# Column recurrence and directional maxima scheduled as one region, with reordered stores and a new opening of the last stage

## The chip, the cores and the metric

The kernel runs on one core of one Trainium2 chip. A core has five engines with their own instruction streams: TensorE (PE, matrix products), VectorE (DVE), ScalarE (ACT, functions of one variable), GpSimd (POOL) and SyncE (SP, which here only issues transfers). Sixteen DMA engines move data between the chip's memory and the core's on-chip memory; a transfer is issued from the instruction stream of SP, ACT or POOL. Engines wait for each other by semaphores. The metric is device time in microseconds (us) of one execution of the whole kernel, given as the median of several runs.

## The reference

The input is an image tensor of 8 × 32 × 256 × 256 (batch, channels, rows, columns) in 32-bit floating point. Four layers follow each other; each adds its result to its input, and each works on an input normalised in 16 groups of channels (`_gn`: mean and variance of an image's two channels over all pixels).

```python
x = x + _L0_conv_ref(_gn(x), w1r, w1i, w2r, w2i, bias)      # spectral convolution, 32 x 32 low modes
x = x + _L1_conv_ref(_gn(x), kernel, 1, 2)                  # 5x5 convolution, one kernel for all channels
x = x + _L2_conv_ref(_gn(x), w_ih, b_ih, w_hh, b_hh)        # recurrence over the columns
x = x + _L3_conv_ref(_gn(x), W, b)                          # running maxima in four directions, 1x1 mix
```

The recurrence goes over the 256 columns from left to right. Column 0 is its own state; for each later one, with `x` the three neighbouring rows of the state before:

```python
r = sigmoid(r_i + r_h); z = sigmoid(z_i + z_h)
n = tanh(n_i + r * n_h)
new = n * z + cur_col * (1.0 - z)
```

The last layer takes the normalised input and its running maxima downwards, upwards, to the right and to the left, and mixes these 5 × 32 channels to 32.

## The kernel before

`forward_and_mix` does the forward transform and the mixing of the modes, and stores spectra in a scratch tensor `smd` in the chip's memory. `inverse_and_conv` transforms back, adds, normalises and convolves, in 16 units (image, half of the channels); its output goes to the scratch tensor `x2d` through `store` (L546 to L559), each half unit in twelve transfers: four groups of rows, each with its inner columns, its first 30 columns and its last columns. It reads its inputs as tiles `xb` (loads on POOL, L388) and `spec` (on SP or ACT, L351 and L353). `statistics` and `keep` make the mean and scale of each group into `stb` (copies, L591) with a power on POOL (L583). After the last unit, `keep(n - 1, statistics(n - 1))` comes before `store(n - 1, 1)`, whose transfers are shared between SP and ACT. The first 8 columns of images 0 to 6 are loaded early into a tile `first` (POOL, L678).

`recurrence` takes the columns in 32 blocks of 8. A column is worked on in two half steps, four images each (510 half steps after column 0). For a block, `load` (L739) brings eight tiles of `x2d` on SP; the load of the last image of `first` is on SP too (L746). `normalise` (L752, ACT) scales and shifts half a block of one image. The statistics reach all partitions by a transpose into `turned` (L726) and become `shift` (L730). In a half step PE forms r, z and n of the gates (`within` L772, `across` L780); ACT takes the two sigmoids (`rs` L847, `zm` L849, `zs` L850) and the tanh (L854), DVE makes n (L848, L853), the product with z (L859) and the new state `hs` (L861), POOL the product with 1 - z (`a`, L856) and the sum with the layer's input (L862), which is written over the raw columns. `running` keeps the running maximum to the right (`fm`, L883) and stores it to the scratch tensor `fwd`; `finish` stores the layer's output to `x3d` and takes its statistics (`bst`, L894). Both stores use `store` (L868 to L875): SP, but POOL for the last block's `fwd`. The order of the whole loop is written out by hand (`manual_schedule`); what lies before and behind is ordered by a scheduler.

`maxima_and_mix` goes over the same 32 blocks from right to left, block 31 first. It loads a block of `x3d` (tile `x3`) and of `fwd` (tile `fw`) on SP (`load`, L999). DVE forms the maxima of pairs of row groups (L1033), their maximum `top` (L1035), two scans down and up the rows (`dq` L1037, `uq` L1039), the maxima `m` (L1041, L1043, L1045), and, between these, the eight steps of the running maximum to the left (`back`, `rv`, a copy at L1029 for the rightmost column and L1031 for the others). PE mixes (L1062), ACT adds the bias while it moves results to the tile `ot` (L1077) and issues its store. Ahead of the loop stand the statistics (L921 to L925, L63 to L71, L950 to L957), the bias `bres` (L980, L981) and the constants `cuts`, `top`, `sel` and `wsum`, all on DVE but for the power (L71, POOL).

Tiles live in pools, which are opened and closed as stages begin and end. Where a pool takes the place of an earlier one, its tiles wait until what was there is done with. Transfers issued by SP and ACT take turns on eight semaphores, so that each waits for the one eight before it.

Of the kernel before, what the change touches and what calls it, by code (L numbers as in the profile page):

```python
# [296 lines left out]
def inverse_and_conv(tc, k, d, smd, xmean, x2d, stb, first):  # L297
# [16 lines left out]
    with ExitStack() as ctx:  # L314
        one = ctx.enter_context(tc.tile_pool(name="a2c", bufs=1))
        xp = ctx.enter_context(tc.tile_pool(name="a2x", bufs=1))
        wk = ctx.enter_context(tc.tile_pool(name="a2w", bufs=2))
        sm = ctx.enter_context(tc.tile_pool(name="a2s", bufs=3))
# [226 lines left out]
        def store(u, ch):  # L545
            b, h = units[u]  # L546
            c0 = 2 * CH * h + CH * ch
            x1, to = x1_of(u, ch), x2d[b, :, :, c0 : c0 + CH].rearrange("w a c q -> w a (c q)")
            for a in range(A):
                r = 32 * a  # L550
                queue = nc.scalar if a % 2 and 2 * u + ch == 2 * n - 1 else nc.sync
                queue.dma_start(
                    out=to[TS + 2 : TS * (NT - 1) + 2, a].rearrange("(t w) n -> w t n", w=TS),
                    in_=x1[r + 2 : r + 30, 2:NT].rearrange("w t c q -> w t (c q)"),
                )
                queue.dma_start(out=to[0 : TS + 2, a], in_=x1[r : r + 30, 1].rearrange("w c q -> w (c q)"))
                queue.dma_start(
                    out=to[TS * (NT - 1) + 2 : W, a], in_=x1[r + 2 : r + 32, 0].rearrange("w c q -> w (c q)")
                )  # L559
# [49 lines left out]
        with tc.manual_schedule(engines=None):  # L609
# [21 lines left out]
            for u in range(n):  # L631
# [47 lines left out]
                if more:  # L679
                    squares(u + 1, 1, 1, 1, NT)  # L680
            keep(n - 1, statistics(n - 1))
            store(n - 1, 1)
# [20 lines left out]
def recurrence(tc, k, d, x2d, x3d, fwd, stb, first, loaded, mean1, mv3):  # L703
# [10 lines left out]
    with ExitStack() as ctx:  # L714
        one = ctx.enter_context(tc.tile_pool(name="bc", bufs=1))
        blk = ctx.enter_context(tc.tile_pool(name="bb", bufs=2))
        wk = ctx.enter_context(tc.tile_pool(name="bw", bufs=2))
# [15 lines left out]
        for t in hs[0] + hs[1]:  # L733
            nc.vector.memset(t, 0.0)
# [4 lines left out]
        def load(bi):  # L739
            if bi:  # L740
                t = blk.tile([P, B, WB, Q], F32, name=f"xw_{bi}", tag="xw", bufs=4)
                for b in range(B):
                    nc.sync.dma_start(out=t[:, b], in_=columns(x2d, b, bi * WB, (bi + 1) * WB))
            else:
                t = first
                nc.sync.dma_start(out=t[:, B - 1], in_=columns(x2d, B - 1, 0, 8))  # L746
            raws[bi] = t
            norms[bi] = blk.tile([P, B, WB, Q], F32, name=f"xn_{bi}", tag="xn")

        def normalise(bi, b, half):  # L750
            w = slice(half * WB // 2, (half + 1) * WB // 2)
            nc.scalar.activation(  # L752
                norms[bi][:, b, w], raws[bi][:, b, w], AF.Identity, bias=shift[:, b : b + 1], scale=sc[:, 1, b : b + 1]
            )
# [71 lines left out]
        def step(w, x):  # L826
# [6 lines left out]
            else:  # L833
# [22 lines left out]
                product = nc.gpsimd.tensor_tensor(a, zm, cur, ALU.mult)  # L856
                if pieces[x]:
# [10 lines left out]
        def store(bi, dst, t):  # L868

            for a in range(A):  # L870
                for b2 in range(2):
                    (nc.gpsimd if bi == NB - 1 and dst is fwd else nc.sync).dma_start(
                        out=dst[bi, :, a, b2].rearrange("(i c) n -> c i n", c=C),
                        in_=t[rows(a), 4 * b2 : 4 * b2 + 4].rearrange("p i w q -> p i (w q)"),
# [14 lines left out]
        def finish(bi):  # L889
            raw = raws[bi]  # L890
            store(bi, x3d, raw)
# [5 lines left out]
        with tc.manual_schedule(engines=None):  # L897
            load(0)
            load(1)
            for half in range(2):  # L900
                for b in range(B):
                    normalise(0, b, half)
            for bi in range(NB):
                for wi in range(WB):
                    if wi == WB // 2 and bi + 2 < NB:
                        load(bi + 2)
                    for x in range(NC):
                        step(bi * WB + wi, x)
                        if bi + 1 < NB:
                            half, b = divmod(NC * wi + x, B)  # L910
                            normalise(bi + 1, b, half)
                    running(bi, wi)
                finish(bi)
# [4 lines left out]
        parts = bst.rearrange("p b n (h k) -> p b (n h) k", k=3)  # L918
        n = 2 * NB
        second = one.tile([P, B, n], F32, name="second")  # L920
        nc.vector.tensor_tensor(second, parts[:, :, :, 1], parts[:, :, :, 1], ALU.mult)  # L921
        nc.vector.scalar_tensor_tensor(second, parts[:, :, :, 2], n / float(W * Q), second, ALU.mult, ALU.add)
        nc.vector.tensor_reduce(mv3[:, :, 0], parts[:, :, :, 1], AX.X, ALU.add)
        nc.vector.tensor_reduce(mv3[:, :, 1], second, AX.X, ALU.add)
        nc.vector.tensor_scalar_mul(mv3, mv3, 1.0 / n)  # L925


def maxima_and_mix(tc, k, d, x3d, fwd, mv3, mean1, out):
# [4 lines left out]
    NB = W // WB  # L933
    with ExitStack() as ctx:
        one = ctx.enter_context(tc.tile_pool(name="cc", bufs=1))
        blk = ctx.enter_context(tc.tile_pool(name="cb", bufs=2))
        op = ctx.enter_context(tc.tile_pool(name="co", bufs=3))
        ps = ctx.enter_context(tc.tile_pool(name="cp", bufs=2, space=PSUM))
# [5 lines left out]


        sta, _ = finish_stats(tc, one, ps, k, mv3, B, k.pair, "c", "o1", 2)
        st = one.tile([P, 2, 2], F32, name="st3")
        for i in range(4):
            q = slice(32 * i, 32 * i + 32)
            nc.vector.tensor_copy(st[q], sta[q, i::4, :])  # L950
        shift = one.tile([P, 2], F32, name="shift3")
        nc.vector.scalar_tensor_tensor(shift, st[:, :, 0], -1.0, st[:, :, 1], ALU.mult, ALU.mult)
        wsc = one.tile([P, 2, 5, C], F32, name="wsc")
        for b2 in range(2):
            nc.vector.tensor_scalar_mul(wsc[:, b2], w3, st[:, b2, 1:2])

            nc.vector.tensor_tensor(wsc[:, b2, 0], wsc[:, b2, 0], k.ident32, ALU.add)  # L957


        wsum = one.tile([P, A, C], F32, name="wsum")  # L960
        nc.vector.tensor_tensor(wsum[:, 0], w3[:, 0], w3[:, 1], ALU.add)
        for t in range(2, 5):
            nc.vector.tensor_tensor(wsum[:, 0], wsum[:, 0], w3[:, t], ALU.add)
        for j in range(1, A):
            nc.vector.tensor_copy(wsum[:, j], wsum[:, 0])
        sel = one.tile([P, 2, 4], F32, name="sel")
        nc.vector.memset(sel, 0.0)
        for i in range(4):
            q = slice(32 * i, 32 * i + 32)
            nc.vector.tensor_copy(sel[q, :, i], shift[q])  # L970
        bp = ps.tile([P, 2, 4], F32, name="bp", tag="o0")
        nc.tensor.matmul(
            bp.rearrange("p b i -> p (b i)"),
            lhsT=wsum.rearrange("p j o -> p (j o)"),
            rhs=sel.rearrange("p b i -> p (b i)"),
            start=True,
            stop=True,
        )
        bres = one.tile([P, 2, 4], F32, name="bres")
        nc.vector.tensor_scalar_add(bres, bp, b3[:, 0:1])  # L980
        nc.vector.tensor_tensor(bres, bres, mean1.rearrange("p (b i) -> p b i", b=2), ALU.add)  # L981


        QP = Q + 2
        cuts = one.tile([P, 2, 2 * WB, QP], F32, name="cuts")
        nc.vector.memset(cuts, BIG)
        nc.vector.memset(cuts[:, 0, :, 0:1], -BIG)
        nc.vector.memset(cuts[:, 1, :, QP - 1 : QP], -BIG)
        cutf = cuts.rearrange("p s w q -> p s (w q)")
        top = one.tile([P, 2, WB, QP], F32, name="top")  # L990
        nc.vector.memset(top, -BIG)

        xs = {}

        def load(bi):

            for src, tag, n in ((x3d, "x3", A + 2), (fwd, "fw", A)):
# [221 lines left out]
```

## Time and profile before

| | us |
|---|---|
| median of 3 runs | 3059.18 |
| lowest and highest run | 3055.52, 3066.23 |
| the profiled execution's own time | 3042.76 |
| its span in the trace | 3041.0 |
| first stage | 0 to 293 |
| first matmul of the convolution's stage | 316.63 |
| last matmuls of that stage's statistics | 997 |
| first sigmoid of the recurrence | 1020.50 |
| last `hs` of the recurrence | 2376.29 |
| first maximum of the last stage (L1033) | 2405.08 |
| from there to the end | 636 |

In the profile, busy times of an engine are sums over its instructions, without those that only wait or issue transfers. "PEclk" or "granted clock" is the share of full speed that PE was given. A row of a timeline has start, duration, engine, line, operation, output and inputs, and in brackets how long the engine had stood before it and what it waited for. A row of the chain has start, length and what the end of the execution hung on in that time; a part called DMA is a transfer under way, "SPq" the issuing of one. The profiled execution is 16.4 us (0.5%) below the median of the runs.

### The profile page before, as it was taken

How to read it: one execution, taken by the hardware profiler on the slowest of the kernel's cores; microseconds unless marked ns; L12 is line 12 of the kernel's file. 1: busy time of each engine (PE TensorE's matmuls, PEld its weight loads, DVE VectorE, ACT ScalarE, POOL GpSimd, SP SyncE). 2: the span in 40 equal slices, each digit the busy share in tenths (PEclk: the TensorE clock that was granted, in tenths of full speed). 3: DMA queues.
4: the chain of work that ended last, by engine and by line, in shares of the span. 5: the costliest groups of instructions: out<-in, count | busy, mean ns of one | idle time of the engine just before them, and what ended most of it. 6: DMA issues, size and time to landing. Idle time of an engine off the chain costs nothing.

```text
span 3041.0 us, 111672 instructions
## 1 busy us (share of the span) xinstructions
PE 2787.3 (92%) x47736; PEld 1644.8 (54%) x47736; DVE 2580.6 (85%) x5172; ACT 1868.2 (61%) x4482; POOL 874.4 (29%) x1253
## 2 busy tenths in 40 slices
PE   7986799999999799999999999999999488888887
PEld 4666344444445466666666666666666233333333
DVE  5753688888888699999999999999999799999997
ACT  3432477777677678888888888888887122222222
POOL 0110022211121355555555555555555200000000
PEclk9995899999999899999999999999999799999988
DMA  9977677877765566566666667656674688888885
GB/s 380 392 282 220 202 223 232 240 230 219 230 209 163 140 152 165 142 141 146 165 160 144 141 146 168 157 141 142 150 168 113 205 325 325 324 326 329 333 332 224
DMA packets 468193, 655.69 MB, mean 216 GB/s; under 512 B 328784, under 2 KB 329696, under 8 KB 441456
## 3 DMA queue, kind: packets, MB, share of 16 engines
q1 hardware_dynamic: 407528, 487.89, 55.1%
q0 software_dynamic: 16784, 84.11, 8.3%
q10 hardware_dynamic: 43384, 76.55, 7.0%
q8 instruction: 374, 6.13, 0.8%
q14 instruction: 123, 1.01, 0.1%
HBM read 371.63 MB, written 272.63 MB: 212 GB/s over the span
## 4 chain that ended last, share of the span: by engine, by line
PE 71%; DVE 20%; issue 4%; DMA 3%; ACT 1%; SPq 0%; POOL 0%; ACTq 0%; DVEq 0%; POOLq 0%
PE r L772 14%; PE z L772 13%; PE vp L498 13%; PE ni L772 7%; PE nh L772 6%; PE up L427 4%; DVE rv L1031 4%; PE yp L131 3%; DVE dq L1037 2%; DVE uq L1039 2%; DVE m L1045 2%; DVE m L1043 2%; DVE m L1041 2%; PE sp L158 2%; PE tp L410 2%
## 5 line engine op out<-in xcount | busy, mean ns | idle before, releaser
L780 PE MATMUL z<-hs,weights 64*64 64x256 f32 x4080 | 539.4, 382 | 0.0
L780 PE MATMUL r<-hs,weights 64*64 64x256 f32 x4080 | 525.4, 375 | 0.0
L780 PE MATMUL ni<-hs,weights 64*64 64x256 f32 x4080 | 524.9, 375 | 0.0
L862 POOL TENSOR_TENSOR xw<-xw,hs 128x256 f32<-128x256 f32 x496 | 339.9, 685 | 635.8 <-DVE hs L861 634.1
L1077 ACT ACTIVATE ot<-o,bres 128x512 f32<-128x512 f32 x256 | 154.9, 688 | 505.5 <-PE o L1062 490.1
L531 DVE SCALAR_TENSOR_TENSOR x<-vp,r,x 128x128 f32<-128x128 f32 (+2 forms) x640 | 350.6, 563 | 90.5 <-PE vp L498 78.2
L498 PE MATMUL vp<-x,c_conv 64*64 64x384 f32 (+5 forms) x4608 | 422.1, 490 | 2.4 <-DVE x L531 2.4
L854 ACT ACTIVATE n<-n,bih 128x256 f32<-128x256 f32 x510 | 259.2, 508 | 187.8 <-DVE n L853 187.8
L856 POOL TENSOR_TENSOR a<-zm,xn 128x256 f32<-128x256 f32 x510 | 372.3, 730 | 6.4 <-ACT zm L849 6.1
L1062 PE MATMUL o<-m,wsc 32*32 32x512 f32 x3072 | 230.5, 728 | 108.7 <-DVE m L1045 103.7
L772 PE MATMUL r<-hs,weights 64*64 64x256 f32 x2040 | 319.0, 389 | 5.1 <-DVE hs L861 4.2
L772 PE MATMUL z<-xn,weights 64*64 64x256 f32 x2040 | 305.3, 376 | 15.2 <-DMA xw<-x2d 15.2
L498 PEld LDWEIGHTS vp<-x,c_conv 64*64 64x64 f32 x4608 | 221.7, 132 | 172.6 <-issue 93.8
L772 PE MATMUL r<-xn,weights 64*64 64x256 f32 x2040 | 305.7, 377 | 0.8 <-ACT rs L847 0.8
L772 PE MATMUL nh<-xn,weights 64*64 64x256 f32 x2040 | 305.7, 376 | 0.0
L772 PE MATMUL z<-hs,weights 64*64 64x256 f32 x2040 | 305.2, 376 | 0.0
L772 PE MATMUL ni<-hs,weights 64*64 64x256 f32 x2040 | 305.2, 376 | 0.0
L752 ACT ACTIVATE xn<-xw,shift,turned 128x256 f32<-128x256 f32 x496 | 290.6, 586 | 0.0
L848 DVE SCALAR_TENSOR_TENSOR n<-nh,bhh,rs 128x256 f32<-128x256 f32 x510 | 246.3, 483 | 45.8 <-ACT rs L847 31.6
L780 PEld LDWEIGHTS ni<-hs,weights 64*64 64x64 f32 x4080 | 284.5, 133 | 0.3
L780 PEld LDWEIGHTS r<-hs,weights 64*64 64x64 f32 x4080 | 281.2, 131 | 0.2
L847 ACT ACTIVATE rs<-r,brz 128x256 f32<-128x256 f32 x510 | 241.3, 473 | 53.1 <-PE r L780 32.5
(166 smaller groups left out, 6245.0 us busy)
## 6 DMA issues: line engine op xcount, KB each, us to landing
xb<-in_xl_dram POOLq DMA_DIRECT2D x96, 768.0 KB, 7.5
xa<-in_xt_dram SPq DMA_DIRECT2D x64, 1024.0 KB
x<-x3d SPq DMA_DIRECT2D x32, 2048.0 KB
fw<-fwd SPq DMA_DIRECT2D x32, 2048.0 KB
out_dram<-ot ACTq DMA_DIRECT2D x64, 1024.0 KB
xw<-x2d SPq DMA_DIRECT2D x248, 256.0 KB
fwd<-fm SPq DMA_DIRECT2D x248, 256.0 KB
x3d<-xw SPq DMA_DIRECT2D x248, 256.0 KB
```

The source lines that it names most:

```text
L498: ins = nc.tensor.matmul(vps[bank][to, :, dst], lhsT=k.conv[r, P : P + 64] if kind == 2 else k.conv[r, o], rhs=pair_of(u, ch, g, lo, hi, s ...
L531: nc.vector.scalar_tensor_tensor(x, src[o], r1[rows, g : g + 1], x, ALU.mult, ALU.add, accum_out=s1[rows, 0, n, ch, g : g + 1])
L752: nc.scalar.activation(norms[bi][:, b, w], raws[bi][:, b, w], AF.Identity, bias=shift[:, b : b + 1], scale=sc[:, 1, b : b + 1])
L772: ins = nc.tensor.matmul(out[r], lhsT=weights[r, kind, gate, :], rhs=src[r], start=start, stop=stop)
L780: ins = nc.tensor.matmul(out[pairs[1 - i]], lhsT=weights[r, kind, gate, :], rhs=prev[r, :, q0 : q0 + Q], start=False, stop=stop,)
L847: rs = nc.scalar.activation(r, p["r"], AF.Sigmoid, bias=brz[:, 0:1])
L848: nc.vector.scalar_tensor_tensor(m, p["nh"], bhh[:, 2:3], r, ALU.add, ALU.mult)
L854: nc.scalar.activation(m, m, AF.Tanh, bias=bih[:, 2:3])
L856: product = nc.gpsimd.tensor_tensor(a, zm, cur, ALU.mult)
L862: nc.gpsimd.tensor_tensor(raw, raw, new, ALU.add)
L1062: nc.tensor.matmul(pts[b2][i][32 * j : 32 * j + 32].rearrange("p (w q) -> p w q", q=Q), lhsT=wsc[q, b2, t, :], rhs=src[j][q, b2], start=first,
L1077: nc.scalar.activation(ot[:, i], pts[b2][i], AF.Identity, bias=bres[:, b2, i : i + 1])
```

## The change

In `inverse_and_conv` the pool `a2c` is opened after `a2x` and `a2w`. `store` issues all its transfers on SP and the first columns ahead of the inner ones; for the last half unit it is ordered by parts, all first columns, then all inner, then all last. It is now called ahead of the statistics, behind a small sigmoid on ACT, and the load of the last image of `first` follows it on POOL.

In `recurrence` the tiles lie in more pools, which wait by the bytes that a tile covers (`reuse_waits="tile"`) and not for the whole of what lay there. Only the edges of `hs` are cleared. `normalise` can go to POOL: the second half of block 0 for images 0 to 3 before the first step, for images 4 to 7 in half steps 2 to 5, and the first half of block 1 for images 0 to 3 in half steps 8 to 11. The last block's `x3d` is stored in three parts (columns 0 to 3, 4 to 5, 6 to 7), and its `fwd` on SP.

The last stage is put into the same hand-ordered region. It loads block 30 first, then block 31 (both on ACT), and begins with maxima of block 30 between the steps of the statistics. Block 31's steps come in between; block 30 is finished before block 31's `m`. From block 29 on the order is that of before. The constants are made on POOL.

```diff
-        one = ctx.enter_context(tc.tile_pool(name="a2c", bufs=1))
         xp = ctx.enter_context(tc.tile_pool(name="a2x", bufs=1))
         wk = ctx.enter_context(tc.tile_pool(name="a2w", bufs=2))
+        one = ctx.enter_context(tc.tile_pool(name="a2c", bufs=1))
...
-                queue = nc.scalar if a % 2 and 2 * u + ch == 2 * n - 1 else nc.sync
...
+            last = 2 * u + ch == 2 * n - 1
+            parts = [(a, part) for a in range(A) for part in range(3)]
+            for a, part in sorted(parts, key=lambda x: x[1]) if last else parts:
+                r, queue = 32 * a, nc.sync
+                if part == 0:
+                    queue.dma_start(out=to[0 : TS + 2, a], in_=x1[r : r + 30, 1].rearrange("w c q -> w (c q)"))
...
+            nc.scalar.activation(junk[:, 0, 0:1], k.mhalf[:, 0:1], AF.Sigmoid)
+            store(n - 1, 1)
+            nc.gpsimd.dma_start(out=first[:, B - 1], in_=columns(x2d, B - 1, 0, 8))
             keep(n - 1, statistics(n - 1))
-            store(n - 1, 1)
...
+        one = ctx.enter_context(tc.tile_pool(name="bc", bufs=1, reuse_waits="tile"))
+        xnp = ctx.enter_context(tc.tile_pool(name="bn", bufs=2, reuse_waits="tile"))
+        xws = {i: ctx.enter_context(tc.tile_pool(name=f"bx{i}", bufs=1, reuse_waits="tile")) for i in (0, 3, 1, 2)}
...
-            nc.vector.memset(t, 0.0)
+            nc.vector.memset(t[:, :, 0 : Q + 2 : Q + 1], 0.0)
...
-                nc.sync.dma_start(out=t[:, B - 1], in_=columns(x2d, B - 1, 0, 8))
...
+            if other:
+                nc.gpsimd.tensor_scalar(
+                    norms[bi][:, b, w], raws[bi][:, b, w], sc[:, 1, b : b + 1], shift[:, b : b + 1], ALU.mult, ALU.add
+                )
+                return
...
                 product = nc.gpsimd.tensor_tensor(a, zm, cur, ALU.mult)
+                if extra:
+                    normalise(*extra, True)
...
-            store(bi, x3d, raw)
+            store(bi, x3d, raw, 6 if bi == NB - 1 else 0)
...
-            for half in range(2):
-                for b in range(B):
-                    normalise(0, b, half)
+            for b in range(B):
+                normalise(0, b, 0)
+            for b in range(BC):
+                normalise(0, b, 1, True)
+            other = {2 + b: (0, BC + b, 1) for b in range(BC)}
+            other.update({8 + b: (1, b, 0) for b in range(BC)})
...
+                    if bi == NB - 1 and wi in (3, 5):
+                        store(bi, x3d, raws[bi], wi - 3 if wi == 3 else 4, wi + 1)
...
-            load(NB - 1)
-            for bi in range(NB - 1, -1, -1):
+            load_x(NB - 2, nc.scalar)
+            load_x(NB - 1, nc.scalar)
+            load_f(NB - 2, nc.scalar)
+            load_f(NB - 1, nc.sync)
+            constants()
+            sums()
+            order("m10")
+            variance()
+            order("m11 m12")
+            scales()
+            order("m13")
+            biases()
+            order("m14 b07 b06 m15 b05 b04 m16 b03 b02")
+            known(NB - 2)
+            order("m00 b01 b00 m01 b17 b16 b15 b14 m02 b13 b12 m03 b11 b10")
+            finish(NB - 2)
+            load_x(NB - 3, nc.sync)
+            load_f(NB - 3, nc.sync)
+            order("m04 m05 m06")
+            known(NB - 1)
+            finish(NB - 1)
+            for bi in range(NB - 3, -1, -1):
```

In a word of `order`, "m" is one of the seven maxima of a block (0: pairs, 1: `top`, 2 and 3: the scans, 4 to 6: the three `m`) and "b" a step to the left; the first digit is the block counted from 31 downwards, the second the maximum or the column. `known` issues the products of four of the five inputs, `finish` those of the maximum to the left, the bias and the output's store.

## The prediction

> **What bounds the kernel now.** I read the page's slices first: PE 9 to 10 tenths through the convolution and the recurrence, DVE and DMA 8 to 9 tenths after it, and dips between. Then busy times by stretch, to put a price on each stage and each dip.
>
> ```profile
> core 0: us, PE busy (x) PEld busy (x) DVE busy (x) ACT busy (x) POOL busy (x), PEclk, DMA share, GB/s
> ...
> 1002.00:1009.00 7.00, 0.00 (x0) 0.00 (x0) 0.37 (x1) 0.00 (x0) 0.00 (x0) 0.50 0.62 164
> ...
> 1100.00:2340.00 1240.00, 1235.65 (x22380) 841.67 (x22376) 1125.09 (x2343) 1024.76 (x2330) 640.91 (x935) 1.00 0.63 149
> ...
> 2397.00:2405.00 8.00, 0.00 (x0) 0.00 (x0) 0.00 (x0) 0.00 (x0) 0.00 (x0) 0.50 0.88 330
> ...
> 2424.00:3010.00 586.00, 487.65 (x9732) 214.33 (x9702) 584.97 (x455) 145.21 (x240) 0.00 (x0) 0.93 0.85 324
> ```
>
> The recurrence is PE's (1235.65 of 1240 us), the last stage DVE's (584.97 of 586). At both seams all engines stand. Nothing in the change shortens a matmul or a maximum; it can win only at seams. The chain and the engines' timelines say what ends them.
>
> ```profile
> 998.95 6.22 DMA x2d<-x
> 1005.18 3.03 DMA x2d<-x
> ...
> 1010.23 8.34 ACT xn L752 x17
> ```
> ```profile
> 1008.63 0.98 DVE L726 STREAM_TRANSPOSE turned<-stb 128x768 f32<-128x768 f32 x1 [8.64 <-DMA x2d<-x]
> ```
> ```profile
> 1019.21 1.28 ACT L847 ACT_TABLE_LOAD   x1
> 1020.50 0.47 ACT L847 ACTIVATE rs<-r,brz 128x256 f32<-128x256 f32 x1
> ```
>
> First seam: the statistics are in stb at 1000.0, but the transpose waits to 1008.63 for the convolution's last stores; then 18 normalise operations and a table load stand ahead of the first sigmoid (rs).
>
> ```profile
> 2384.17 12.70 DMA x3d<-xw
> ...
> 2397.08 7.78 DMA x<-x3d
> ```
> ```profile
> 2392.71 0.17 DVE L981 TENSOR_TENSOR bres<-bres,mean 128x8 f32<-128x8 f32 x1
> 2405.08 2.29 DVE L1033 TENSOR_TENSOR x<-x 128x2048 f32<-128x2048 f32 x1 [12.20 <-DMA x<-x3d]
> ```
>
> Second seam: DVE's statistics end at 2392.88, then it waits 12.2 us for the last block to go to memory (landed 2397) and come back (7.8).
>
> **The change, part by part,** on the profiled execution (3042.76; span 3041.0). It lies 16.4 us under the median of the runs, 3059.18; I take the gain off both alike.
>
> *Pools of the convolution.* The six xb loads no longer wait for the stage before to have stored; they issue at about 292.2, PE's last matmul there, instead of 298.65. The last smd store (293.93 on SP) then shares the DMA engines with them, and SP has bias and spec queued behind it; PE's next matmul is at 316.63, after spec. The trace's packets price both ends: beside xb, the 128-byte packets of spec pass at 64 to 80 per us, alone at 900 to 1000, so spec moves only once xb is through, whoever goes first. xb frees the engines 6.4 us earlier, about 307.5, and spec alone takes 8.7: 316.2. Gain 0.5; ends +4 (smd not starved) and -2 (smd landing late and 2 us of issue behind).
>
> *First seam.* The last unit's stores go with the first columns first (four of 61 KB instead of 256 columns), all on SP, ahead of the statistics. The load of first's last image moves from SP to POOL, where it now stands **in front of the last power**: POOL waits for those four stores. They issue from about 996 and land about 1000 (999.5 to 1004, since older stores of 400 KB share the queue). Then the issue 0.9 (the seven loads of first on POOL have a mean of 895 ns), the power 1.67, stb 0.2, transpose 0.98, shift 0.1: normalising starts at 1004.6, not 1010.23, for the transpose no longer waits for the other stores. Behind it 8 operations stand ahead of the first sigmoid (8 × 0.50 = 4.0 us), not 18. What ends next is PE: its r of the first half step, hidden before under the normalising, was through its last matmuls at 1018.5 (1017.88 + 0.38, and z's between), 8.3 us after normalising began, at a granted clock of 0.50 to 0.64. The seam's hs memsets (8 × 0.28 on DVE) lay under the normalising too. So rs, 0.2 after r, at 1004.6 + 8.5 = 1013.1 instead of 1020.50, and the steps behind it as much earlier: **7.4**. Ends: 3 (first columns at 1004, the rest as above) and 9 (at 999.5, and PE a microsecond quicker).
>
> The table load is worth nothing beside that: left where it was, it would end at 4.0 + 1.28 = 5.3 us, ahead of r. The statistics' four waits now sit on POOL; behind them stand only the power and the raw adds, which need the normalised columns anyway. SP, relieved of the load of first, goes straight on to block 1's loads.
>
> The eight other halves and the first four of block 1 (12 operations) go to POOL, four at the start, eight inside half steps, each before the raw add (L862), which has idle time before it of 635.8 us / 496 = 1.28.
>
> ```profile
> L862 POOL TENSOR_TENSOR xw<-xw,hs 128x256 f32<-128x256 f32 x496 | 339.9, 685 | 635.8 <-DVE hs L861 634.1
> L856 POOL TENSOR_TENSOR a<-zm,xn 128x256 f32<-128x256 f32 x510 | 372.3, 730 | 6.4 <-ACT zm L849 6.1
> ```
>
> POOL's only operation of that kind in the trace (L358, 64x1024) takes 2776 ns; a quarter is 0.69. I take 0.74, nearest to the two rows above: hidden. With that cover gone, 2.78 each, it costs 8 × (2.78 - 1.28) = 12.
>
> Two rules of the Trainium skill speak here. That 64x1024 operation takes DVE 0.69 us and POOL 2.78, 4.0 times as long; "GPSIMD Engine Reference", 3.1, keeps "use DVE for elementwise" as the rule, against this move, with a ratio of 1.96 and 1.03 cycles an element at 1.2 GHz for bodies of up to two operations. By that an operation here would be an estimated 0.22 us, a third of the row's; the sum is 21.3 by either, as both fit into the idle time. The table load's row has 1.28 us, with rs 0.01 behind; "ScalarE: Activation LUTs", What ACT_TABLE_LOAD costs, puts a drain of 1.38 on top. By the page a load left in place would end at 4.0 + 2.66 = 6.7 us, still ahead of r, so the sum stays 21.3 by that too.
>
> *Second seam.* DVE's statistics end at 2386.22 as before. Constants leave DVE for POOL (idle here). ACT, idle after the last tanh at 2375.7, loads block 30, stored long ago: a load's bytes take 5 us and issue to use 8.0 (2397.08 to 2405.08), so it is there by 2384.3, under the statistics. The last block's stores are cut in three; only two columns (0.5 MB) are left at the end. Stored about 2387, loaded from 2387.4, in hand at 2396 to 2400. The fwd stores move from POOL to SP; each DMA there also waits for the one eight before it, on SP or ACT, so some wait for block 30's load, the last for block 31's: landed about 2408.5 (2400, plus 5 for the fwd load of block 30 ahead of it, plus 3 as the chain's 3.03 for a store). Behind them on SP stands only block 31's load of fwd, and behind ACT's waiting loads only evictions of block 30, not due before 2410.
>
> DVE, by starts from its timeline: block 30's pair maxima 2386.3 + 2.2; variance 0.8; top 1.1; scan 2.3 (its tile needs the last stores landed, due 2390.4, there 2387); scales 2.1; scan 2.3; biases 0.4; m 2.2: 2399.7. Now block 31's copy (0.3) needs the reload: just there. Seven backward maxima at 0.6, m, m, pair maxima and top (2.2, 2.2, 2.2, 1.1) with that copy: 2411.9. Block 30's backward tile lies where the fwd stores read, landed 2408.5: free. Its eight maxima at 0.6 and two scans at 2.3: 2421.3; three m at 2.2: 2428.0. Block 29's tile is block 30's, so its load is issued at 2421.4 and usable 8.0 to 8.6 later: a **new stall of about 2 us**, then one more copy (0.4). Block 29 so starts in effect at 2430.4. Before: 2405.08 + 2 × 19.38 = 2443.84. Gain **13.4**; ends 8 (reload at 2405, or the fwd stores holding DVE 5 us) and 15 (no stall).
>
> The other 29 blocks and the tail are as before, 19.38 us each by DVE; PE's instructions are the same ones. In the recurrence the loads and stores on SP keep their order.
>
> Sum: 0.5 + 7.4 + 13.4 = **21.3**; profiled execution 3042.8 to 3021.5, median 3059.2 to 3038.
>
> **Rivals.**
> 1. *Seam two gives half back.* 16 KB packets of loads beside 2 KB and smaller ones of stores: the fwd stores or block 31's reload come 8 us later than I have them, and block 30's own tail waits. For it: 16 KB packets last 611 ns against 84 to 153 for those of stores. Against: DVE has 20 us of block 30's and constant work before it needs either. 3038 + 8 = 3046.
> 2. *Seam one doesn't do what it says.* Power and transpose still end late, since the first columns' stores sit behind the 400 KB of the unit before on SP. For it: in the run before, SP's last stores took from 995 to 1008. First columns at 1004 or later: gain 3 instead of 7.4, 3042; with rival 1, 3050.
> 3. *The half step grows: slower.* Place: the 510 half steps between 1021 and 2376, now with tiles in new pools and other addresses; DVE is busy 1125 of 1240 us there and carries the chain from rs to hs. Price 510 × the growth: from 42 ns the gain is gone, from 60 ns the kernel is slower by 0.3%; 100 ns give 3089. Against: the same operations, shapes and order on each engine, with as many waits.
> 4. *Better than forecast*: smd not starved (+4) and no stall at block 29 (+2): 3031.
>
> **How the numbers follow.** Forecast (3038 ± 6) 0.55; rival 4 0.10; rival 1 0.12; rival 2, with or without 1, 0.10; rival 3 and its lesser forms 0.13, of which half ends slower. 0.3% is 9 us, about what a measurement can tell from no change: faster means under 3050. Faster 0.55 + 0.10 + 0.12 + 0.06 = 0.83; same 0.10; slower 0.07. Range: ends of the parts' gains, 4 + 9 + 15 = 28, and -2 + 3 + 8 = 9: 3031 to 3050; opened to 3029 and 3054 for rivals 2 and 3 in their small forms.
>
> **What the profile after would show.** Right: the transpose at about 1003 with a POOL releaser and no x2d store in front; a table load between 996 and 1004; rs near 1013; POOL's new tensor_scalar near 0.74; the first pair maxima near 2386.3 and DVE near full to 2421; a gap of about 2 us ahead of block 29's; then blocks 19.38 apart; y on PE at 316. Wrong: rs after 1017 (rival 2), DVE idle by 5 us or more between 2395 and 2421 (rival 1), a half step over 2.69 us against 2.65 (rival 3), or POOL's new operations over 1.28 us.

## The result and the profile after

The changed kernel takes 3024.59 us (median of 4 runs, 3017.64 to 3029.68), the kernel before 3057.35 beside it (4 runs, 3050.65 to 3066.23): ratio 0.9884, 95% interval 0.986 to 0.9907, some 33 us less. The forecast was 3038, 21.3 less, and its range ended at 3029: right in direction, too small by 11 us.

The two profiled executions differ by much less, 3041.0 to 3027.8, 13.2 us. So the first thing to do is to cut both into the same stretches. This table does it for two profiles of each kernel (the second ones are the first two runs further down); each number is the distance between two rows of the trace.

| stretch | before | after | difference of the means |
|---|---|---|---|
| start to the first sum of the convolution's input (first L436) | 328.1, 330.1 | 328.8, 331.8 | +1.1 |
| convolution (to the end of the last L498) | 665.1, 678.9 | 672.8, 669.5 | -0.9 |
| to the last statistics copy (`st`) | 3.9, 3.9 | 4.4, 3.9 | +0.2 |
| that copy to the first sigmoid | 23.3, 23.3 | 16.1, 15.4 | -7.6 |
| first sigmoid to that of half step 16 | 36.9, 36.8 | 38.4, 38.6 | +1.7 |
| block 2 (half steps 32 to 48) | 46.6, 46.6 | 42.6, 42.7 | -4.0 |
| whole recurrence, first sigmoid to last `hs` | 1355.8, 1355.7 | 1353.0, 1353.5 | -2.5 |
| last `hs` to the third scan down | 71.8, 72.0 | 60.1, 60.1 | -11.9 |
| third scan to the 32nd | 562.0, 562.1 | 562.0, 562.1 | 0 |
| from there to the end | 30.8, 30.7 | 30.9, 29.4 | -0.6 |

What is the same in every execution sums to -22 (-7.6 - 2.5 - 11.9), or -21.3 with the three small rows. That this meets the forecast's 21.3 is in part luck: the second seam gives less than was forecast, and two changes inside the recurrence that the forecast did not have (-4.0 in block 2, +1.7 in block 0) make up for it. The rest of the 33 us must lie for the most part in the one stretch whose length changes much from execution to execution, the convolution. Busy times by stretch of the changed kernel:

```profile
core 0: us, PE busy (x) PEld busy (x) DVE busy (x) ACT busy (x) POOL busy (x), PEclk, DMA share, GB/s
...
1100.00:2340.00 1240.00, 1239.36 (x22464) 844.90 (x22460) 1126.02 (x2340) 1029.95 (x2337) 643.22 (x936) 1.00 0.63 149
...
2385.00:2397.00 12.00, 3.90 (x57) 1.71 (x68) 11.61 (x24) 0.00 (x0) 2.59 (x1) 0.50 1.03 386
2397.00:2426.00 29.00, 14.54 (x307) 5.38 (x287) 28.65 (x26) 2.42 (x4) 0.00 (x0) 0.76 0.46 167
```

PE's 1235.65 of 1240 us have become 1239.36: there were 4 us of idle time inside the recurrence, and I had read that row as full. At the second seam DVE now works where it stood 12.2 us. The first seam, on DVE, POOL and ACT (start, duration, engine, line, what, and the wait ahead):

```profile
1005.86 0.17 DVE L582 COPY st<-s 128x16 f32<-128x16 f32 x1 [2.26 <-PE s L574]
...
1011.95 0.17 DVE L595 COPY stb<-st 128x16 f32<-128x16 f32 x1 [5.23 <-POOL st L587]
1012.16 0.98 DVE L734 STREAM_TRANSPOSE turned<-stb 128x768 f32<-128x768 f32 x1
```
```profile
1009.35 0.88 POOL L687 DMA_DIRECT2D first<-x2d  x1 [13.25 <-DMA x2d<-x]
1010.25 1.67 POOL L587 TENSOR_TENSOR st<-ve,c_mhalf 128x8 f32<-128x8 f32 x1
```
```profile
1013.45 4.04 ACT L764 ACTIVATE xn<-first,shift,turned 128x256 f32<-128x256 f32 x8 [7.20 <-DVE shift L738]
1021.93 0.47 ACT L859 ACTIVATE rs<-r,brz 128x256 f32<-128x256 f32 x1 [4.44 <-PE r L792]
```

The transpose follows the power at once, and the power waits behind the load, as foreseen. The first sigmoid comes 8.5 us after normalising began, which was the figure used. Second seam, DVE:

```profile
2384.74 2.35 DVE L1075 TENSOR_TENSOR x<-x 128x2048 f32<-128x2048 f32 x1
...
2398.36 0.42 DVE L1068 COPY rv<-x 128x512 f32<-128x512 f32 x1
...
2429.86 2.29 DVE L1075 TENSOR_TENSOR x<-x 128x2048 f32<-128x2048 f32 x1 [1.97 <-DMA x<-x3d]
```

No wait between the statistics and 2428, and then the stall of 2 us ahead of block 29.

### The profile page after: what moved, and what is told of

Its sections match the earlier page's. It is cut to its first block, busy times and chain, and to the rows that moved or that the text cites. A ratio compares the mean times of both kernels' runs of the same rounds, so it can differ in the third digit from the quotient of the medians.

```text
span 3027.8 us, 111688 instructions
## 1 busy us (share of the span) xinstructions
PE 2784.2 (92%) x47736; PEld 1643.4 (54%) x47736; DVE 2578.6 (85%) x5161; ACT 1864.6 (62%) x4471; POOL 886.4 (29%) x1270
## 4 chain that ended last, share of the span: by engine, by line
PE 66%; DVE 19%; issue 4%; DMA 2%; ACT 1%; SPq 0%; POOL 0%; DVEq 0%; ACTq 0%; POOLq 0%
PE r L784 14%; PE z L784 13%; PE vp L498 12%; PE ni L784 7%; PE nh L784 7%; DVE rv L1070 4%; PE up L427 4%; DVE dq L1085 2%; DVE uq L1087 2%; DVE m L1096 2%; DVE m L1093 2%; DVE m L1090 2%; PE tp L410 2%; PE mp L269 2%; PE o L1102 1%
## 5 line engine op out<-in xcount | busy, mean ns | idle before, releaser
L498 PE MATMUL vp<-x,c_conv 64*64 64x384 f32 (+5 forms) x4608 | 424.2, 490 | 7.9 <-DVE x L531 7.9
L498 PEld LDWEIGHTS vp<-x,c_conv 64*64 64x64 f32 x4608 | 222.2, 132 | 179.5 <-issue 101.5
```

The lines of the kernel that those rows point to most:

```text
L498: ins = nc.tensor.matmul(vps[bank][to, :, dst], lhsT=k.conv[r, P : P + 64] if kind == 2 else k.conv[r, o], rhs=pair_of(u, ch, g, lo, hi, s ...
```

## The experiments

Twelve experiments, in three sets of four; each set shared one chip and its runs of the kernel before, to which the ratios refer. The time given first is the median of the experiment's own runs.

**Both kernels again.** Theory A: the sum for the seams was right, the surplus lies in a convolution of changing length. Theory B: something is shortened in every execution.

> The kernel before, unchanged. Theory A (the seams gain the 21 us that were predicted; what was measured beyond that is a convolution stage whose length differs from execution to execution): the stretches of the two seams are as in the first profile within 1 us (last statistics of the convolution to first sigmoid 23.3; last hs to the third scan 71.8), the convolution (first L436 to last L498) is not 665 again but anything from 665 to 685, and the ratio is 1.000 within 0.003. Theory B (the change shortens a stage that was never its subject, in every execution): all stretches repeat within 1 us, the convolution at 665.

> The changed kernel, unchanged. Theory A: seams 16.1 and 60.0 again within 1.5 us; convolution between 660 and 680, not 672.8 again; over more executions the gain shrinks from 33 us towards 21, a ratio near 0.993. Theory B: ratio 0.989 again, the convolution 672.8 again.

Before: 3055.34 (12 runs, 3042.38 to 3062.3), ratio 1.001 (0.9994 to 1.0026); seams as in the table, the convolution 678.9 instead of 665.1. After: 3019.67 (4 runs), 0.9881 (0.9867 to 0.9896). So A is right that seams are fixed and the convolution is not, and wrong that the gain would shrink: two sets of runs give 33 us. The convolution must be shorter on average, in a way that two profiles each don't show.

Most of its 16 units take 41.3 to 41.6 us, some 2 to 7 more, and which ones changes from execution to execution. What stands there is DVE, ahead of L436, mostly for a store of the convolution's output whose buffer it is about to write (waits of DVE over the whole convolution, then of SP's queue in one unit, both of the kernel before in its second profile: total, times, longest):

```profile
DVE x L436 <- DMA x2d<-x: 9.3, 2, 5.0
```
```profile
SPq L556 <- DMA spec<-smd: 8.9, 1, 8.9
```
```profile
403.29 0.51 ACTq L351 DMA_DIRECT2D spec<-smd  x1
403.85 0.60 ACTq L353 DMA_DIRECT2D spec<-smd  x1
404.49 7.20 ACTq L353 DMA_DIRECT2D spec<-smd  x1
```
```profile
415.46 0.45 SPq L552 DMA_DIRECT2D x2d<-x  x1
424.85 0.32 SPq L556 DMA_DIRECT2D x2d<-x  x1
```

SP issues seven of a store's twelve transfers and then stands 8.9 us: the eighth takes, in turn, the semaphore of the spectrum's load on ACT's queue. That load's packets pass slowly beside xb (138 of them in the 2 us from 416, beside 90 packets of xb; 919 in the 2 us from 422, beside none). Where it lands late, the rest of the store is late, and L436 can be. It need not be: of the profiles below, that of the run with the power ahead of the load has 23.9 us of this wait of SP, and its DVE never stands for a store.

**The order of the stores.** The changed kernel with the old order (for all half units but the last), and the kernel before with the new one, as the only edits:

```diff
-            parts = [(a, part) for a in range(A) for part in range(3)]
+            parts = [(a, part) for a in range(A) for part in ((0, 1, 2) if last else (1, 0, 2))]
```

> The changed kernel with the convolution's stores in the order of before (inner, first, last columns) for all half units but the last. In the changed kernel's profile DVE waits three times, 13.7 us in sum, for such a store before it writes x (L436); before, 0.9. If the order of the stores makes that wait: it goes to about 1 us, the convolution to 665 and the time falls by up to 8 us, ratio 0.986. If it is scatter (theory A): the wait is anything from 0 to 14 us in either order, and the ratio that of the changed kernel run beside it within 0.003.

```diff
+                queue.dma_start(out=to[0 : TS + 2, a], in_=x1[r : r + 30, 1].rearrange("w c q -> w (c q)"))
                 queue.dma_start(
                     out=to[TS + 2 : TS * (NT - 1) + 2, a].rearrange("(t w) n -> w t n", w=TS),
                     in_=x1[r + 2 : r + 30, 2:NT].rearrange("w t c q -> w t (c q)"),
                 )
-                queue.dma_start(out=to[0 : TS + 2, a], in_=x1[r : r + 30, 1].rearrange("w c q -> w (c q)"))
```

> The kernel before with one edit: in every store of the convolution the first columns go ahead of the inner ones. So far the kernels with the new order have run at 3022 on average, 4 to 5 us over their stall-free time, the changed kernel with the old order at 3028.6, 11 over, and the kernel before (old order) at 3053, 13 over its own. Theory S (the order lowers the number of stalls in the convolution): 6 to 8 us less, ratio 0.9975. Theory N (the order does nothing, those differences are scatter): ratio 1.000 within 0.0015. The seams keep their lengths (23.3 and 71.8).

Old order in the changed kernel: 3028.66 (6 runs), 0.9915 (0.9901 to 0.9929), against 0.9881 for the changed kernel beside it: 9 to 10 us given back, and the two intervals do not overlap. My expectation had the sign wrong; it took the old order for the better one. New order in the kernel before: 3044.78 (12 runs), 0.9979 (0.9964 to 0.9995): 6.4 us gained, theory S. In its profile no DVE wait for x2d is left, and SP's waits for the spectrum's loads are (total, times, longest)

```profile
SPq L553 <- DMA spec<-smd: 5.6, 3, 2.8
```

against, in the kernel before's second profile,

```profile
SPq L556 <- DMA spec<-smd: 49.8, 6, 9.1
```

This wait is in all fourteen profiles (two of each kernel and ten of the other experiments). The four with the old order have 30.5, 49.8, 34.8 and 26.2 us of it, mean 35; the ten with the new order 0.9 to 28.6, mean 14. What it comes to in DVE can be counted too. Apart from waits for PE's L427, which every execution has, DVE stands for more than half a microsecond ahead of L436 ten times in the four profiles with the old order, 9.6 us in each on average, and six times in the ten with the new order, 2.7 us on average. The convolution takes 671.2 us on average in the four and 664.6 in the ten. So the order's worth is seen in the stage itself, at about the size that the times show. Ten of these sixteen waits name a store, five ACT's squares (L453, 4.1 to 6.3 us) and one PE; whether these six have the same origin stays open. Why the order helps the spectrum's load is argued, not shown: with 61 KB instead of 401 KB first, and a wait of 2 us ahead of the second transfer, the small packets have the engines to themselves a little longer.

**The spectrum's load one group earlier.**

```diff
-                        if g == 2:
+                        if g == 1:
                             load_spectrum(units[u + 3][0])
```

> The changed kernel with the load of the next image's spectrum issued one group of the convolution (5 us) earlier. Theory L: the convolution stalls because SP's stores wait, in order, for the semaphore of that load, whose 128-byte packets pass slowly beside xb; then the store that L436 needs is late. With 5 us more for the load SP goes on earlier: DVE's waits at L436 for x2d fall to 2 us or less, the convolution is 661 to 664, the time 3017 to 3019 with little scatter, ratio 0.987. If the stall has another cause (the bandwidth of the stores alone): nothing changes, ratio as the changed kernel's, 0.988 to 0.990, and waits of 3 to 14 us remain in some profiles.

3024.17 (5 runs), 0.991 (0.9892 to 0.9928); one wait of 2.7 us at L436 in its profile, SP's wait for the load still 11.7 us. But the edit did not give the 5 us that I expected of it. In all six units that load a spectrum, ACT issues the first part of it 14.25 us after the unit's first L498, against 15.6 in the changed kernel: 1.3 us sooner. So the run decides between neither branch, and that the spectrum's load is what makes DVE stand rests on the waits alone.

**The convolution's pools.**

```diff
+        one = ctx.enter_context(tc.tile_pool(name="a2c", bufs=1))
         xp = ctx.enter_context(tc.tile_pool(name="a2x", bufs=1))
         wk = ctx.enter_context(tc.tile_pool(name="a2w", bufs=2))
-        one = ctx.enter_context(tc.tile_pool(name="a2c", bufs=1))
```

> The changed kernel with the convolution's pools opened in the order of before (a2c first). By the prediction's price this part is worth 0.5 us (ends 4 and -2): xb issues at about 298.5 again, spec lands near 316.5, and the ratio is that of the changed kernel within 0.003. Theory B, if it is this part that gains beyond the seams: the time rises by 10 us or more, ratio 0.992 against 0.989 for the changed kernel beside it, and the convolution stage is longer by as much.

3028.41 (4 runs), 0.9913 (0.99 to 0.9926), 10 us over the changed kernel beside it. Not for xb (the stretch to the first L436 is 328.9), and not in the convolution, which took 662.0, as short as any. ACT:

```profile
1008.33 4.04 ACT L764 ACTIVATE xn<-first,shift,turned 128x256 f32<-128x256 f32 x8 [12.61 <-DMA x2d<-x]
```

`shift` was there at 1002.6. ACT waits for the stores of x2d, so with the old order of pools the tile that normalising writes must lie where the last half unit's stores still read. The start comes 13.0 us after the statistics instead of 7.6 or 8.2, and the first sigmoid 20.5 after them instead of 16.1 or 15.4. So this edit is part of the first seam's gain, worth 5 us there in this profile. The remaining 5 of the 10 are within the scatter of 4 runs of each.

**The power ahead of the load; four operations from POOL to ACT; both by way of ACT.**

```diff
-            nc.gpsimd.dma_start(out=first[:, B - 1], in_=columns(x2d, B - 1, 0, 8))
             keep(n - 1, statistics(n - 1))
+            nc.gpsimd.dma_start(out=first[:, B - 1], in_=columns(x2d, B - 1, 0, 8))
```

> The changed kernel with the load of the last image of first behind the power on POOL. In the changed kernel's profile the power's input was ready at 1006.6, but POOL stood until 1009.35 for that load's wait, and issued it until 1010.23. My reading: normalising starts 3.3 us sooner after the statistics (4.8 instead of 8.1), and the first sigmoid 2.7 sooner, as the last image then comes a little late. Rival: the tiles that normalising writes wait for the stores of the inner columns anyway; then the start moves by less than 1 us.

Normalising began 4.1 us after the statistics (4.8 expected), but the first sigmoid, expected 2.7 us sooner, came 16.4 after them, no better than 16.1 and 15.4, and block 0 takes 39.6 us, 1 more. POOL got to the load only behind its own normalising, and it landed behind the inner columns:

```profile
1001.17 3.55 ACT L764 ACTIVATE xn<-first,shift,turned 128x256 f32<-128x256 f32 x7 [3.75 <-DVE shift L738]
1010.75 0.60 ACT L764 ACTIVATE xn<-first,shift,turned 128x256 f32<-128x256 f32 x1 [6.02 <-DMA first<-x2d]
```

3022.11 (4 runs), 0.9905 (0.9886 to 0.9924).

```diff
+            for b in range(BC):
+                normalise(0, BC + b, 1)
-            other = {2 + b: (0, BC + b, 1) for b in range(BC)}
-            other.update({8 + b: (1, b, 0) for b in range(BC)})
+            other = {8 + b: (1, b, 0) for b in range(BC)}
```

> The changed kernel with four of its twelve normalise operations on POOL (images 4 to 7, second half) moved to ACT, ahead of the first sigmoid. Block 0's half steps (first sigmoid to that of half step 16) take 38.4 us in the changed kernel against 36.85 before; half steps 2 to 5, which have those operations on POOL, carry 1.1 of the difference. If POOL's extra work makes it: 37.3 us, and the first sigmoid not later by more than 0.2, as ACT is done 6 us after it begins and r is ready at 8.3. If it has another cause (late loads of block 1): 38.4 stays.

First sigmoid 13.9 us after the statistics, block 0 at 38.0 instead of 38.4 and 38.6: 0.5 of the 1.1 that were expected. 3019.47 (4 runs), 0.9902 (0.9884 to 0.9919). What else lengthens block 0 stays open; the other four operations on POOL are one candidate.

```diff
+            for i, (a, part) in enumerate(sorted(parts, key=lambda x: x[1]) if last else parts):
+                if last and i == A:
+                    LOADED[:] = [nc.scalar.dma_start(out=first[:, B - 1], in_=columns(x2d, B - 1, 0, 8))]
...
+            if bi == b == half == 0:
+                tc.add_manual_dep(ins.ins, LOADED[0].ins.name, BEHIND, reason="the load is issued first")
...
-            nc.gpsimd.dma_start(out=first[:, B - 1], in_=columns(x2d, B - 1, 0, 8))
```

The edit ahead of this one is in this kernel too.

> norm_act, and the load of the last image of first issued by ACT ahead of its normalising, between the first and the inner columns of the last store; POOL's power then waits for nothing but its input. Last statistics to first normalise 4.2 us (8 in the changed kernel), first sigmoid 3 us sooner if the load lands within 6 us of its issue, block 0 at 37.3: together 4 us less than the changed kernel, ratio 0.987. Rival: the load lands late behind the inner columns, as it did with the power first (5.4 us from issue), and takes back 2 of the 3 us.

Normalising 4.1 us after the statistics, the first sigmoid 12.2: 3.5 less than in the changed kernel, with a wait of 2.0 for the load. 3017.88 (6 runs, one of them 3032.97), 0.9901 (0.9881 to 0.9921). The seam is the shortest of all, but the interval reaches to the changed kernel's 0.9881: scatter like the convolution's is larger than 3.5 us. I don't call it faster.

**The second seam: opening, small last store, or both.** First block 31 opens again:

```diff
...
-            load_x(NB - 2, nc.scalar)
             load_x(NB - 1, nc.scalar)
-            load_f(NB - 2, nc.scalar)
             load_f(NB - 1, nc.sync)
             constants()
             sums()
-            order("m10")
             variance()
...
-            order("m14 b07 b06 m15 b05 b04 m16 b03 b02")
...
-            for bi in range(NB - 3, -1, -1):
+            for bi in range(NB - 1, -1, -1):
```

> The changed kernel with the last stage opened by block 31 as before (statistics, then block 31, no work of block 30 ahead); the three-part store, the constants on POOL and the pools stay. By the prediction's account the gain of this seam comes from DVE working on block 30 while block 31 goes to memory and back: last hs to third scan 70 us (60 in the changed kernel, 72 before), time up by 10 to 12 us, ratio 0.992. Rival: the smaller last store and the pools bring half of it: 65 us, ratio 0.990.

Last `hs` to third scan: 60.3 us, against 60.05. 3020.14 (4 runs), 0.9896 (0.9874 to 0.9918). Both guesses fall: beside the other edits, the opening with block 30 is worth 0.2 us. ACT's queue and DVE show why:

```profile
2373.12 0.39 ACTq L1039 DMA_DIRECT2D x<-x3d  x1
```
```profile
2383.80 0.17 DVE L1028 TENSOR_TENSOR bres<-bres,mean 128x8 f32<-128x8 f32 x1
2384.26 2.29 DVE L1073 TENSOR_TENSOR x<-x 128x2048 f32<-128x2048 f32 x1 [0.29 <-DMA x<-x3d]
```

The reload is issued 6.1 us after the last `hs` (2367.05), when the last two columns are stored, and 11 us later it ends as the statistics do. There is no stall left to fill. Then the other way round, block 30 first and the last store whole:

```diff
-            store(bi, x3d, raw, 6 if bi == NB - 1 else 0)
+            store(bi, x3d, raw)
...
-                    if bi == NB - 1 and wi in (3, 5):
-                        store(bi, x3d, raws[bi], wi - 3 if wi == 3 else 4, wi + 1)
```

> The changed kernel with the last block's x3d stored whole at its end, as before; block 30 still opens the last stage. With block 31 first and the three-part store, last hs to third scan was 60.3 us, as with block 30 first (60.1). Theory P (the small last store is what gains; the opening adds nothing to it): the stores land about 21 us behind the last hs, as before, the reload 8 to 11 later, block 31's copy, due at 23.5, waits 6 to 8 us, and the stretch is 66 to 68. Theory O (the opening covers a late store too, either edit alone is enough): 60 to 62.

61.8 us: theory O. ACT issued its two loads (the second one block 31's) from 2364.40 to 2379.52, so the whole store had landed 14 us after the last `hs` (2365.19), not 21. Here the stores of `fwd` come behind it on SP, where the kernel before issues them beside it on POOL; that this is why it lands sooner is not shown. DVE's copy of block 31 waits little:

```profile
2364.40 15.12 ACTq L1037 DMA_DIRECT2D x<-x3d  x2
```
```profile
2390.16 0.43 DVE L1066 COPY rv<-x 128x512 f32<-128x512 f32 x1 [1.42 <-DMA x<-x3d]
```

3020.65 (4 runs), 0.991 (0.9886 to 0.9934). Last, the three-part store alone, in the kernel before (the removed lines above, put in there):

> The kernel before with the last block's x3d stored in three parts, and nothing else of the change. Theory P: the last two columns land some 6 us behind the last hs, the reload lies under DVE's statistics, last hs to third scan falls from 72 to 60.5, the ratio is 0.9962 (11.5 us). Theory O: the part of the gain that belongs to the opening and to the loads on ACT is missing, 65 us or more, ratio 0.998.

66.1 us, half of the gain; 3041.44 (12 runs), 0.9966 (0.9952 to 0.9981), 10 us, of which this seam has 5.8, the lower end of the interval. The chain there:

```profile
2385.53 3.87 POOL fwd L872 x7
2389.41 8.51 DMA fwd<-fm
...
2398.34 7.83 DMA x<-x3d
```

The reload no longer waits for the stores of x3d but for those of `fwd`, presumably as its tile takes the place of one that they read. So: three parts alone 66.1, with the pools that wait by bytes and the loads on ACT 60.3, block 30 first with a whole store 61.8, both 60.05, and the kernel before, with none of it, 71.8. Beside the new pools and the loads on ACT, either edit nearly closes the gap, and the second finds nothing left. What those pools and loads are worth without either edit was not run.

**The 4 us inside the recurrence** can be read from the profiles; no run changes them alone. In both profiles of before, half step 32 takes 6.38 us, its neighbours 2.6 to 2.9, and DVE and ACT (first profile) show what lies there:

```profile
1100.10 1.82 DVE L986 MEMSET cuts<- 128x2112 f32 x1 [0.41 <-issue]
1101.84 0.36 DVE L861 TENSOR_TENSOR hs<-n,a 128x256 f32<-128x256 f32 x1
1102.83 0.19 DVE L961 TENSOR_TENSOR wsum<-w 128x32 f32<-128x32 f32 x1 [0.63 <-DMA w<-in_w3T_dram]
...
1103.89 0.94 DVE L991 MEMSET top<- 128x1056 f32 x1 [0.16 <-issue]
```
```profile
1105.14 0.51 ACT L854 ACTIVATE n<-n,bih 128x256 f32<-128x256 f32 x1 [4.27 <-DVE n L853]
```

The scheduler had put the last stage's constants into block 2, on the engine that carries the chain of a half step. In the changed kernel, with the last stage in the hand-ordered region, they are on POOL behind the recurrence, and half step 32 takes 2.59 us.

## Why the prediction was right or wrong

- **Pools, 0.5.** The price is small, but the step failed. xb is issued 0.6 us after PE's last matmul of the stage before, as I had it (6.5 in the kernel before). But spec does not land sooner for it. SP's load of the bias, which stands ahead of spec's in its queue, waits for the last store of smd, now under way beside xb. The next transfer on SP follows 14.8 us behind that store; in the kernel before it was 3.4.

```profile
SPq L322 <- DMA smd<-sm: 14.4, 1, 14.4
```

  spec's first load is issued at 310.38 instead of 297.70, and PE waits 25.5 and 25.4 us for spec where it waited 24.5 and 24.9. That is the lower end of my range, "smd landing late", at 0.7 us instead of 2. What the edit is worth lies at the first seam: 5 us, inside the 7.4 that I had put down to the stores, the load and the power.
- **First seam, 7.4.** Measured 7.6, by the steps named: load, then power, transpose 6.3 us after the statistics, normalising 7.6 to 8.2 after them (7.4 forecast), r 7.2 to 8.5 later (8.5 forecast). That a wait stands in front of the power was right, but taking it out alone gains nothing.
- **POOL's normalising, hidden.** "I take 0.74 ... hidden" was too kind. The four ahead of the steps take 0.55 us each, those inside half steps 0.55 to 1.25, and block 0 is 1.7 us longer; moving four of them back recovered 0.5.
- **"Constants leave DVE for POOL (idle here)", at nothing.** Here the step failed: I placed them at the second seam without looking where the trace has them. They cost 4.0 us in block 2, and the row with 1235.65 of 1240 showed it.
- **Second seam, 13.4.** Measured 11.9, with the stall of 2 us (1.97), the extra copy (0.42) and DVE busy in between. The 1.5 that are missing are DVE's own: from block 30's pair maxima to block 31's last m my sum has 41.7 us, the trace 43.15 (2384.74 to 2427.89). The account of DVE is right for this program, but not as a cause: without the opening the seam is as short.
- **The order of the stores in all half units.** The step that made the forecast wrong. "The last unit's stores go with the first columns first" is all the prediction says of an edit that applies to every store of the convolution. I priced the one store at the seam and left the other 31 without a price. It is worth 6.4 us alone (1.5 to 11 by the interval), and 9 to 10 in the changed kernel; DVE's stalls ahead of L436, which my sum left as they were, are 9.6 us in an execution with the old order and 2.7 with the new.
- **The basis.** "I take the gain off both alike" assumed that the 16.4 us between the profiled execution and the median were a matter of the run. For the most part they were stalls of the convolution, which a change can remove: the second profile of before is 15.8 us longer than the first, and 13.8 of these are in the convolution. The first had one of its short ones, 665.1.
- **Rivals.** 1 did not happen: DVE never waited for `fwd` or block 31. 2 did not: the first columns had landed by 1009.35, 4.3 us after the first of their stores was issued (1005.07). 3 did not: blocks in the middle of the recurrence take 42.3 to 42.7 us in both. 4, "better than forecast", was the side on which it fell, but for neither of its reasons: smd's store was starved (14.4 us), and the stall at block 29 was there.

The numbers together: -7.6 (first seam) + 1.7 (block 0) - 4.0 (constants) - 11.9 (second seam) is -21.8; the convolution, 6 to 10, brings it to -28 to -32, and the runs have -33 (28 to 43 by the interval). The 1 to 5 us that are left are within it.

## What to carry to other kernels

Cut two or three executions into stretches before pricing a change: what scatters between them may be a stall that some edit can remove or make, and one profile shows it by luck. Look in the trace whether an edit moved what it was meant to move: a load placed one group (5 us) earlier in the program was issued 1.3 us earlier. An edit inside a loop or helper is priced for every call, not for the call it was made for. A few us of idle time in a row that looks full are worth a look at the timeline: a scheduler may have put work of another stage there.

## What the runs showed of the hardware that was not expected

- A load of 128-byte packets on one queue can hold up another queue's stores without sharing a byte: they share semaphores in turn, and SP stood for it six times in one execution, 49.8 us in sum and 9.1 at most.
- POOL's operation of two scalars on 128x256 takes 0.55 us where DVE stands, 0.55 to 0.58 where DVE makes only the product L873 in that time, and 0.83 to 1.26 where the new state (L875) or the running maximum (L897) falls into it (both profiles of the changed kernel). In the first of them the means are 0.699 over the eight on block 0 and 0.971 over the four on block 1:

```profile
L760 POOL TENSOR_SCALAR xn<-first,turned,shift 128x256 f32<-128x256 f32 x8 | 5.6, 699 | 1.6 <-DVE shift L738 1.6
L760 POOL TENSOR_SCALAR xn<-xw,turned,shift 128x256 f32<-128x256 f32 x4 | 3.9, 971 | 0.0
```

  The 0.22 us estimated ahead from the Trainium skill's 1.03 cycles an element ("GPSIMD Engine Reference", 3.1) are below all of them.
- A memset of 128x2112 takes POOL 1.88 us and DVE 1.82, one of 128x1056 0.98 and 0.94: for filling a tile there was little to choose between them here.
